# Perceiver layer on one core: the first 512 context rows by seven half-size products instead of eight

## The chip, the cores and the metric

The kernel runs on one core of one Trainium2 chip. Its time is the device time of one execution in microseconds (us), as the median of several runs. The engines are called as the profile calls them: PE (TensorE, matrix products), PEld (its weight loads), DVE (VectorE), ACT (ScalarE), POOL (GpSimd) and SP (SyncE, which issues most DMAs here). All values are 32-bit floats. The profile counts every matrix product of that type as two matmul records; "record" below means one of the two.

## The reference, cut to what matters

One layer is computed on 256 tokens of width 512 (`x`): cross attention with 4096 further context rows, then a state-space block, then a mixture of 32 experts. Only the first part is touched:

```python
xn   = layernorm(x)                                  # 256 x 512
q    = rope(rms_norm(xn @ wq)); k0 = rope(rms_norm(xn @ wk)); v0 = xn @ wv
k_c  = rms_norm(h_ctx_kv @ wk_ctx)                   # 4096 x 512: 4 heads of 128
v_c  = h_ctx_kv @ wv_ctx                             # 4096 x 512
out  = softmax(q [k0; k_c]^T / sqrt(128), causal on the first 256) [v0; v_c] @ wo
```

The context is worked through in eight steps of 512 rows. In each step a 512 x 512 block of context is multiplied by the two 512 x 512 matrices `wk_ctx` and `wv_ctx`, side by side a 512 x 1024 matrix.

## The kernel before

**Two ways to multiply a context step.** Steps 1 to 7 (`fast_steps`, line 398) use Winograd's form of Strassen's method, in two levels: both matrices are cut into halves each way, and seven products of halves take the place of eight, at the price of sums of blocks ahead of them and of results behind them. Step 0 (`context_pieces`, line 310) multiplies plainly: per 128 rows one `key_piece` and one `value_piece`, each four products of 128x128 by 128x512 accumulated in one PSUM bank (`project`, line 222), 32 products in all. A key piece is copied out by ACT, its squares are summed by ACT (`head_squares`) for the norm, and TensorE turns it (`key_transpose`, line 299). The norm factor is not multiplied into the key but used as the scale of the later exponential (this is the `bounded` arm of the program, the one that runs).

**The opening.** SP issues the loads of the first context block `ctx0`, of `wk_ctx` (`wkc`), `x`, the rest of `ctx0` and `wv_ctx` (`wvc`); then, behind a branch, `wk`, `wq`, `wv` and two further context blocks. While they land, PE makes three key pieces, turns the layer-normed `xn` (`turn_xn`, line 213; DVE copies the result to `xT`, line 220), makes a value piece and goes on to the self blocks.

**The self blocks.** `self_block` (line 562) makes 512 columns of k or q for 128 tokens: eight records on PE into one of two `ps_mm` banks; ACT copies them to one of two `raw` buffers (line 536) and sums squares; DVE does the rotary embedding in four instructions (lines 541 to 544); POOL raises the norm factor to the power -1/2 (line 200) and multiplies it in (line 545); DVE transposes 32x32 blocks (line 268) and DMAs put them in place. The two blocks of `wq[3]` are turned by PE instead (line 575). There are ten such blocks. One list after line 607 sets the order in which they, the value pieces and the transposes are written; a planner then gives each engine the earliest-written instruction that it takes to be ready, so the order can shift a little. Each engine works its queue in order.

**Sums of the weights.** The fast steps need T1, T2 and T4, sums of quarters of the weights. POOL makes them in three instructions of 128x1024 (`weight_sums`, lines 338 to 340) once `wvc` is there. The fourth, T3, is formed in place in `wvc` by DVE (`last_sum`, line 389) in the middle of the attention to the layer's own tokens, when the value pieces of step 0 no longer need `wvc`; POOL then makes four further sums of it (`second_sums("wv")`, lines 379 to 382).

**Attention.** `bounded_attention` (line 652) goes through the sources s = 0 (own tokens), 1 (context step 0) to 8. Beside s = 1 run the products of context step 1, and so on, so each step is ready before it is attended to.

Of the kernel before, what the change touches and what calls it, by code (L numbers as in the profile page):

```python
# [11 lines left out]
FP = mybir.dt.float32  # L12
# [7 lines left out]
P = 128  # L20
# [55 lines left out]
def perceiver_layer(ctx: ExitStack, tc: tile.TileContext, a: dict, out: bass.AP):  # L76
# [24 lines left out]
    load_wkc(1, 1)  # L101
    load_wkc(2, 2)
    nc.sync.dma_start(x_sb, a["x"].rearrange("(t p) d -> p t d", p=P))
    load_ctx0(1, 1)
    load_ctx0(2, 2)
    nc.sync.dma_start(wvc, a["wv_ctx"].rearrange("(k p) n -> p k n", p=P))

# [33 lines left out]
    def layer(ctx, bounded):  # L141
# [71 lines left out]
        def turn_xn(t, tp, halves=False):  # L213

            for k in range(KD):
                TE.transpose(tp[:, k * P:(k + 1) * P], xn[:, t, k * P:(k + 1) * P], ident)

            for copy, ks in (((V.tensor_copy, slice(0, KD // 2)), (S.copy, slice(KD // 2, KD))) if halves else
                             ((V.tensor_copy, slice(0, KD)),)):
                copy(xT[:, ks, t * P:(t + 1) * P], tp.rearrange("p (k n) -> p k n", k=KD)[:, ks])  # L220

# [20 lines left out]

        ctx_tiles = {0: ctx0}

        def load_ctx(c):
            ct = ctxp.tile([P, CK // P, KD, P], FP, tag="ctx", name="ctx")
            nc.sync.dma_start(ct, a["ctxT"][c])
            ctx_tiles[c] = ct

        wk = wpiece(a["wk"], "wk")  # L250
        wq = [wpiece(a["wq"][:, 0:512], "wq0")]
        wv = wpiece(a["wv"], "wv")
        wq += [wpiece(a["wq"][:, j * 512:(j + 1) * 512], f"wq{j}") for j in range(1, 4)]
        load_ctx(1)

# [31 lines left out]
        def context_tiles(c):  # L287

            kT = kvp.tile([P, NKV, CK], FP, tag="kT", name="kT")
            v = kvp.tile([P, CK // P, NKV * HD], FP, tag="v", name="v")  # L290
            r = small.tile([P, CK // P, NKV], FP, tag="rk", name="rk", bufs=2)
            kv[c + 1] = (kT, v, r)
            raws = {}

            def key_transpose(i):
                tp = ps_tp.tile([P, NKV, P], FP, tag="tp", name="kTp")
                raw = raws.pop(i)
                for h in range(NKV):
                    TE.transpose(tp[:, h, :], raw[:, h, :], ident)

                if bounded:
                    S.copy(kT[:, :, i * P:(i + 1) * P], tp)
                else:
                    S.activation(kT[:, :, i * P:(i + 1) * P], tp, AF.Copy, scale=kw_col)

            def key_blocks(i):
                turn_heads(kT[:, :, i * P:(i + 1) * P], raws.pop(i), kd[c][i])
            return v, r, raws, key_transpose, key_blocks

        def context_pieces(c):  # L310

            ct = ctx_tiles.pop(c)
            v, r, raws, key_transpose, _ = context_tiles(c)

            def key_piece(i):
                ps = ps_mm.tile([P, 512], FP, tag="mm", name="ps_k")
                project(ps, lambda k: ct[:, i, k, :], lambda k: wkc[:, k, :])
                raws[i] = raw = krp.tile([P, NKV, HD], FP, tag="kraw" if i == 1 else "kn", name="kraw")
                S.copy(raw, ps.rearrange("p (h d) -> p h d", d=HD))
                key_rms(raw, r[:, i, :])  # L320

            def value_piece(i):
                ps = ps_mm.tile([P, 512], FP, tag="mm", name="ps_v")
                project(ps, lambda k: ct[:, i, k, :], lambda k: wvc[:, k, :])
                S.copy(v[:, i, :], ps)

            return [[lambda i=i, f=f: f(i) for i in range(CK // P)] for f in (key_piece, value_piece, key_transpose)]

# [54 lines left out]

        def last_sum():

            V.tensor_tensor(b12, b22, b12, ALU.subtract)
            each(second_sums("wv"))  # L390

        three = ring([(ps_mm, "mm"), (ps_mm, "mm"), (ps_tp, "tp")] if bounded else [(ps_mm, "mm")])

        def fast_steps(c, behind=None):
# [19 lines left out]
            def sums():  # L414
# [3 lines left out]
                G.tensor_tensor(S2, S1, a11, ALU.subtract)  # L418
                left("P6", S2)
                G.tensor_tensor(S3, a11, a21, ALU.subtract)  # L420
                left("P7", S3)
# [108 lines left out]

        heads_done = []

        def norm_rope(ps, t, tb):
# [9 lines left out]
            V.tensor_tensor(u[:, :, HALF:HD], raw[:, :, 0:HALF], sn[:, :, HALF:HD], ALU.mult)  # L543
            V.tensor_tensor(o, o, u, ALU.add)
            heads_done.append(G.tensor_tensor(o, o, r.unsqueeze(2).to_broadcast([P, REP, HD]), ALU.mult).ins)
# [5 lines left out]
        kv[0] = (kT0, v0, None)  # L551
        ctx_k, ctx_v, ctx_t = context_pieces(0)
        for t in range(NT):
            normed = layernorm(t)
        for i in range(3):
            ctx_k[i]()
        for t in range(NT):
            turn_xn(t, ps_sc.tile([P, 512], FP, tag="sc", name="lnT"))
        rope_table(tab_k, kw_bc)
        rope_table(tab_q, qw_bc)  # L560
        with tc.issue_after(normed.ins):
# [25 lines left out]
        q = [[lambda j=j, t=t: q_of(j, t) for t in range(NT)] for j in range(4)]  # L587
        turns = ctx_t[0:3]

        def last_key():  # L590
            ctx_k[3]()
            return ctx_t[3]

# [3 lines left out]
        def behind_head(group, n=1):  # L597
            with tc.issue_after(heads_done[-1]):
                for _ in range(n):
                    next(early[group])  # L600

        weights_of = lambda: next(placed)
        one, two = lambda: behind_head("t"), lambda: behind_head("t4", 2)
        for f in (ctx_v[0], lambda: k_of(0), lambda: k_of(1), last_key, *q[0], ctx_v[1], weights_of, lambda: self_value(0),
                  q[1][0], one, q[1][1], one, lambda: self_value(1), weights_of, q[2][0], one, q[2][1], one, ctx_v[2],
                  q[3][0], two, q[3][1], two, ctx_v[3]):
            turn = f()
            if f not in (weights_of, one, two):
                turns.append(turn)
            while len(turns) > 2:  # L610
                turn = turns.pop(0)
                if turn:
                    turn()
# [19 lines left out]
        pin(nc.sync.dma_start(by_channel, a["by_channel"]))  # L633
        pin(nc.sync.dma_start(by_head, a["by_head"].partition_broadcast(P)))

# [16 lines left out]
        def bounded_attention(beside):  # L652

            pp = pool("pp", 4)
            bq = small.tile([P, 3], FP, tag="bq", name="bq", bufs=1)
            V.tensor_reduce(bq[:, 0:1], qw_bc, AX.X, ALU.max, apply_absolute_value=True)
            V.tensor_reduce(bq[:, 1:2], kw_bc, AX.X, ALU.max, apply_absolute_value=True)
            shift = bq[:, 2:3]
# [49 lines left out]
            for s in range(NC + 1):  # L708
# [12 lines left out]
                for n, st in enumerate(steps):  # L721
                    if s == 0 and n == 3:
                        for turn in turns:
                            turn()
                    if s == 0 and n == 8:
                        with tc.issue_after(masked[-1]):
                            last_sum()
                    pending.append((*st, scores(*st)))
# [19 lines left out]
        def general_attention():  # L748
            with ExitStack() as gctx:
# [12 lines left out]
                for turn in turns:  # L762
                    turn()
                last_sum()

                for s in range(NC + 1):
# [1048 lines left out]
```

## Time and profile before

| what | value |
|---|---|
| runs | 960.70, 960.75, 959.02 us; median 960.7 |
| the profiled execution | 961.0 us, of which the span of the profile is 959.2 |
| busy over the span | PE 98%, DVE 60%, POOL 45%, ACT 40% |
| granted TensorE clock | 0.998 of full |
| first matmul record of PE | at 5.45 us |
| first score of the attention | at 79.34 us |
| first product of context step 1 | at 101.14 us |

Times are counted from the start of the span. In a line of the timeline the first number is the start, the second the duration of a merged group of equal instructions, "x8" their number, and what stands in brackets is the idle time of the engine ahead of it and what ended it. Full-size matmul records overlap in the listing: each is shown with 592 ns, though the next begins 429 ns later.

### The profile page before, as it was taken

To read this page: it belongs to the slowest core of one execution; us is meant where nothing else is said; L and a number is where in the kernel's file an instruction comes from. 1 tells how busy PE (TensorE), PEld (TensorE's weight loads), DVE (VectorE), ACT (ScalarE), POOL (GpSimd) and SP (SyncE) were. 2 spreads that over 40 slices of the span, in tenths; PEclk is the share of its full clock that TensorE was granted. 3 is DMA by queue.
4 is the path that set the end of the run, shared out by engine and by line. 5 is a ranking of instruction groups with operands and counts; after the bars stand their busy time and mean duration, and the time that the engine had idled before them with its cause. 6 is when DMAs were issued, how large, how long until landed. Compare 5 with 4: busy or idle time off the path is not lost.

```text
span 959.2 us, 10117 instructions
## 1 busy us (share of the span) xinstructions
PE 939.9 (98%) x3025; PEld 508.0 (53%) x3025; DVE 571.4 (60%) x1205; ACT 383.0 (40%) x872; POOL 429.3 (45%) x487
## 2 busy tenths in 40 slices
PE   7999999999999999999999999999999999999996
PEld 3444555555555555555555555544465655555442
DVE  4458766566566656665756656658497666632223
ACT  3646444344344444343443444443253742122221
POOL 3559956345444644634724723300013234545542
PEclk9999999999999999999999999999999999999999
DMA  9732053053034015104205203360046453899983
GB/s 328 241 78 47 0 176 87 1 154 89 1 86 141 15 35 174 35 14 152 77 1 153 67 1 88 81 228 0 0 157 209 165 196 122 327 328 366 362 322 109
DMA packets 130803, 124.93 MB, mean 130 GB/s; under 512 B 80017, under 2 KB 99250, under 8 KB 125490
## 3 DMA queue, kind: packets, MB, share of 16 engines
q1 hardware_dynamic: 119216, 77.96, 26.9%
q0 software_dynamic: 7904, 40.90, 11.7%
q10 hardware_dynamic: 3618, 5.33, 1.5%
q8 instruction: 26, 0.43, 0.2%
q14 instruction: 39, 0.32, 0.1%
HBM read 88.76 MB, written 35.41 MB: 129 GB/s over the span
## 4 chain that ended last, share of the span: by engine, by line
PE 95%; issue 1%; POOL 1%; DVE 1%; DMA 1%; ACT 0%; SPq 0%; POOLq 0%; DVEq 0%
PE oT L693 24%; PE scT L668 24%; PE ps_kv L459 15%; PE ps_egu L225 5%; PE ps_self L225 4%; PE ps_v L225 2%; PE ps_o L892 2%; PE ps_xbc L225 2%; PE ps_k L225 2%; PE ps_ye L1616 2%; PE ps_out L1089 1%; PE ps_z L225 1%; PE ps_sgu L225 1%; PE ps_ye L1619 1%; PE xgTp L1495 1%
## 5 line engine op out<-in xcount | busy, mean ns | idle before, releaser
L684 DVE TENSOR_TENSOR lacc<-lacc,prT 128x512 f32<-128x512 f32 x256 | 200.6, 785 | 197.3 <-ACT prT L674 196.2
L674 ACT ACTIVATE prT<-scT,bq,rk 128x512 f32<-128x512 f32 x256 | 198.4, 775 | 280.4 <-PE scT L668 269.5
L668 PE MATMUL scT<-qT,kT 128*128 128x512 f32 x536 | 273.5, 592 | 0.0
L693 PE MATMUL oT<-prT,v 128*128 128x512 f32 x528 | 269.4, 592 | 0.1
L693 PEld LDWEIGHTS oT<-prT,v 128*128 128x128 f32 x528 | 100.1, 190 | 125.8 <-issue 117.9
L668 PEld LDWEIGHTS scT<-qT,kT 128*128 128x128 f32 x536 | 101.2, 190 | 41.0 <-issue 30.6
L459 PE MATMUL ps_kv<-fast,ctx 128*128 128x256 f32 x350 | 99.6, 379 | 0.0
L459 PEld LDWEIGHTS ps_kv<-fast,ctx 128*128 128x128 f32 x350 | 66.4, 190 | 48.3 <-issue 39.9
L410 POOL TENSOR_TENSOR ctx<-ctx 128x128 f32<-128x128 f32 x21 | 11.4, 542 | 98.7 <-PE ps_kv L459 98.7
L200 POOL TENSOR_TENSOR rk<-pv,mhalf 128x4 f32<-128x4 f32 x32 | 37.4, 1180 | 28.0 <-DVE pv L199 28.0
L262 ACT ACTIVATE xn<-kraw 128x128 f32<-128x128 f32 x112 | 33.5, 301 | 39.4 <-POOL kraw L434 22.1
L459 PE MATMUL ps_kv<-wkv,ctx 128*128 128x256 f32 x168 | 48.9, 379 | 0.0
L444 POOL TENSOR_TENSOR v<-fast,v 128x768 f32<-128x768 f32 x21 | 40.9, 1960 | 16.2 <-DVE fast L488 15.6
L459 PEld LDWEIGHTS ps_kv<-wkv,ctx 128*128 128x128 f32 x168 | 31.8, 190 | 28.4 <-issue 25.0
L699 DVE TENSOR_TENSOR oacc<-oT,oacc 128x512 f32<-128x512 f32 x64 | 43.6, 682 | 0.0
L1599 DVE TENSOR_TENSOR hid<-si,ps_egu 128x128 f32<-128x128 f32 x18 | 5.2, 287 | 47.5 <-ACT si L1597 47.5
L459 PE MATMUL ps_kv<-fast,fast 128*128 128x256 f32 x112 | 33.3, 379 | 0.0
L459 PEld LDWEIGHTS ps_kv<-fast,fast 128*128 128x128 f32 x112 | 21.3, 190 | 17.8 <-issue 12.0
L268 DVE STREAM_TRANSPOSE tr<-kraw 128x512 f32<-128x512 f32 x28 | 18.3, 690 | 19.6 <-POOL kraw L433 19.6
L892 PE MATMUL ps_o<-wo,qT 128*128 128x512 f32 x64 | 28.8, 592 | 0.0
L1290 POOL DMA_INDIRECT xg_sb<-xg,place x16 | 15.1, 947 | 29.1 <-PE xgTp L1495 26.7
L225 PE MATMUL ps_self<-wq,xT 128*128 128x512 f32 x64 | 28.1, 592 | 0.0
(439 smaller groups left out, 1412.8 us busy)
## 6 DMA issues: line engine op xcount, KB each, us to landing
xg<-xn SPq DMA_DIRECT2D x6, 2560.0 KB, 9.4
ctx<-in_ctxT_dram SPq DMA_DIRECT2D x7, 1024.0 KB, 5.0
kd<-tr SPq DMA_DIRECT2D x112, 64.0 KB, 2.2
kT<-kd SPq DMA_DIRECT2D x28, 256.0 KB, 3.0
ye<-y_sb ACTq DMA_DIRECT2D x19, 256.0 KB, 8.3
wq<-in_wq_dram SPq DMA_DIRECT2D x4, 1024.0 KB, 14.4
wo<-in_wo_dram SPq DMA_DIRECT2D x4, 1024.0 KB, 7.9
w_in<-in_W_inT_dram SPq DMA_DIRECT2D x4, 1024.0 KB, 8.7
```

The costliest lines, as they stand in the source:

```text
L200: return G.tensor_tensor(dst, v[:, :n], mhalf[:, :n], ALU.pow)
L225: TE.matmul(ps, lhs(k), rhs_of(k), start=(k == 0), stop=(k == KD - 1))
L262: S.activation(sq[:, h, :], raw[:, h, :], AF.Square, accum_out=ss[:, h:h + 1])
L444: G.tensor_tensor(to[:, 1:4], q, base[:, 1:4], ALU.add)
L459: TE.matmul(b[n], sets[name][i], y, start=start, stop=True, skip_group_check=True)
L668: scored.append(TE.matmul(sc, kT[:, g, i * P:(i + 1) * P], qT[:, t, heads4(g), :].rearrange("p h q -> p (h q)"), start=True, stop=True).ins)
L674: S.activation(pr, sc, AF.Exp, bias=shift, scale=SCALE if r is None else r[:, i, g:g + 1])
L684: V.tensor_tensor(la, la, pr, ALU.add)
L693: TE.matmul(outs[g, t], v[:, i, g * HD:(g + 1) * HD], pr, start=(n == 0), stop=last)
L699: V.tensor_tensor(ov, outs.pop((g, t)), ov, ALU.add)
L892: TE.matmul(m["ps_o", t], aT[:, t, h, :], wo[j][:, h % 4, :], start=(h == 0), stop=(h == NH - 1))
L1616: TE.matmul(ps[i], h[:, i, :], wd[i], start=True, stop=False)
```

## The change

Step 0 also uses seven products of halves, but in one level only. With the context block cut into a11, a12 (rows 0 to 255), a21, a22 (rows 256 to 511) and the weights into b11, b21 (`wkc`) and b12, b22 (`wvc`), the new `first_step` forms

- S1 = a21 + a22, S2 = S1 - a11, S3 = a11 - a21, S4 = a12 - S2 on DVE, in a tile `first_sums` that is taken from the two context buffers;
- P1 = a11 b11 and P2 = a12 b21 (their sum is the key of rows 0 to 255, and P1 is also copied out by ACT), P6 = S2 T2, P7 = S3 T3, P4 = a22 T4, P5 = S1 T1, P3 = S4 b22, each as two groups of two products of 128x128 by 128x512.

Ten additions on DVE (one operand in PSUM, one in SBUF) put the results together. P1 and P2 come first, in the opening; the turns of their two keys are written behind the first and the second self block; P6, P7, P4 and the pair P5, P3 are written into the list of self blocks in the places where value pieces stood. T3 is formed behind the rotary embedding of the fourth self block. The turns of keys use the score banks (`ps_sc`, three) in place of the one `ps_tp` bank.

The opening loads become: `ctx0` rows 0 to 127, `wkc` quarters 0 and 1, `ctx0` rows 128 to 255, `x`, `wkc` quarters 2 and 3, and behind the branch the other half of `ctx0`, `wk` in two halves, `wvc`, then as before. Because `first_sums` holds a context buffer, the load of context step 2 moves from the opening to a place behind the load of `by_head`, at the beginning of s = 1. The rotary tables, the sums S1 to S4 and two small reductions are queued behind the copy of `xT`. `second_sums("wv")` is written among the sums of context step 1.

```diff
     load_wkc(1, 1)
-    load_wkc(2, 2)
+    load_ctx0(1, 1)
     nc.sync.dma_start(x_sb, a["x"].rearrange("(t p) d -> p t d", p=P))
-    load_ctx0(1, 1)
-    load_ctx0(2, 2)
-    nc.sync.dma_start(wvc, a["wv_ctx"].rearrange("(k p) n -> p k n", p=P))
+    load_wkc(2, 1)
+    load_wkc(3, 1)
...
+        load_ctx0(2, 2)
+        wk = wpool.tile([P, KD, 512], FP, tag="w", name="wk")
+        for k in (0, 2):
+            nc.sync.dma_start(wk[:, k:k + 2, :], a["wk"][k * P:(k + 2) * P, :].rearrange("(k p) n -> p k n", p=P))
+        nc.sync.dma_start(wvc, a["wv_ctx"].rearrange("(k p) n -> p k n", p=P))
...
+            def product(ps, lhs, rhs, j, start=True):
+                for k in range(2):
+                    TE.matmul(ps, lhs[:, j, k, :], rhs[:, k, :], start=(start and k == 0), stop=(k == 1),
+                              skip_group_check=True)
+                return ps
...
+            def p1(j):
+                x[j] = product(bank(True), a11, b11, j)
+                S.copy(v[:, j, :], x[j])
+
+            def p2(j):
+                product(x[j], a12, b21, j, False)
+                S.copy(flat(key(j)), x.pop(j))
+
+            def p6(j):
+                V.tensor_tensor(v[:, j, :], product(bank(), S2, T2, j), v[:, j, :], ALU.add)
+
+            def p7(j):
+                V.tensor_tensor(v[:, 2 + j, :], product(bank(), S3, b12, j), v[:, j, :], ALU.add)
+
+            def p4(j):
+                V.tensor_tensor(flat(key(2 + j)), product(bank(), a22, T4, j), v[:, 2 + j, :], ALU.add)
+                return key_done(2 + j)
+
+            def p5(j):
+                z[j] = product(bank(True), S1, T1, j)
+                V.tensor_tensor(v[:, 2 + j, :], z[j], v[:, 2 + j, :], ALU.add)
+
+            def p3(j):
+                product(z[j], S4, b22, j, False)
+                V.tensor_tensor(v[:, j, :], z.pop(j), v[:, j, :], ALU.add)
+
+            def sums12():
+                V.tensor_tensor(S1, a21, a22, ALU.add)
+                V.tensor_tensor(S2, S1, a11, ALU.subtract)
+
+            def sums34():
+                V.tensor_tensor(S3, a11, a21, ALU.subtract)
+                V.tensor_tensor(S4, a12, S2, ALU.subtract)
...
-        for i in range(3):
-            ctx_k[i]()
+        for f in (p1, p2) if bounded else ():
+            for j in range(2):
+                f(j)
...
+        with tc.issue_after(turned.ins):
+            key_turns = [key_done(j) for j in range(2)] if bounded else []
+            rope_table(tab_k, kw_bc)
+            rope_table(tab_q, qw_bc)
+            sums12()
+            sums34()
...
-        for f in (ctx_v[0], lambda: k_of(0), lambda: k_of(1), last_key, *q[0], ctx_v[1], weights_of, lambda: self_value(0),
-                  q[1][0], one, q[1][1], one, lambda: self_value(1), weights_of, q[2][0], one, q[2][1], one, ctx_v[2],
-                  q[3][0], two, q[3][1], two, ctx_v[3]):
+        for f in (*of_heads[0:1], *key_turns[0:1], *of_heads[1:2], *key_turns[1:2], *q[0], weights_of,
+                  lambda: self_value(0), last_first, q[1][0], one, *both(p6), q[1][1], one, lambda: self_value(1), weights_of,
+                  *both(p7),
+                  q[2][0], one, q[2][1], one, *both(p4), q[3][0], two, q[3][1], two, *both(p5), *both(p3)):
...
-            while len(turns) > 2:
+            while len(turns) > 3:
...
-                    if s == 0 and n == 8:
-                        with tc.issue_after(masked[-1]):
-                            last_sum()
```

## The prediction, made before the changed kernel had run

> **What bounds the kernel now.** I read the page first: busy tenths in 40 slices, then the chain of work that ended last.
>
> ```profile
> PE   7999999999999999999999999999999999999996
> ...
> PE 95%; issue 1%; POOL 1%; DVE 1%; DMA 1%; ACT 0%; SPq 0%; POOLq 0%; DVEq 0%
> ```
>
> PE is busy in every slice and the chain is PE's own queue. A matmul record that goes away shortens the span by its pitch, unless PE then waits for something. So I looked at the stretches around the change, and at what PE waits for in the first 100 us:
>
> ```profile
> 5.45:17.87 12.42, 12.42 (x26) 5.52 (x27) 5.93 (x21) 5.56 (x19) 2.15 (x3) 1.00 1.02 367
> 17.87:79.34 61.47, 61.47 (x164) 28.26 (x163) 34.79 (x62) 34.15 (x121) 36.42 (x32) 1.00 0.58 167
> 79.34:101.14 21.80, 21.69 (x55) 9.12 (x54) 19.04 (x23) 14.94 (x24) 21.54 (x21) 1.00 0.18 40
> ```
>
> ```profile
> PE ps_k L225 <- DMA wkv<-in_wk_ctx_dram: 5.4, 1, 5.4
> ```
>
> Columns of the first: stretch, its length, then busy time and count of PE, PEld, DVE, ACT, POOL, the granted clock, the DMA share, GB/s. From 5.45 us on PE has no idle time until the attention; its one wait is the first load. DVE and POOL have 35 and 36 us of work in the 61 us of the self blocks, so there is room, but they take turns in one chain per block. The timeline shows the pitch and the ends that matter:
>
> ```profile
> 5.45 12.42 PE L225 MATMUL ps_k<-wkv,ctx 128*128 128x512 f32 x24 [5.45 <-DMA wkv<-in_wk_ctx_dram]
> ...
> 65.17 3.60 PE L225 MATMUL ps_v<-wkv,ctx 128*128 128x512 f32 x8
> 68.61 7.03 PE L225 MATMUL ps_self<-wq,xT 128*128 128x512 f32 x16
> 75.47 3.60 PE L225 MATMUL ps_v<-wkv,ctx 128*128 128x512 f32 x8
> ...
> 79.34 2.74 PE L668 MATMUL scT<-qT,kT 128*128 128x512 f32 x6
> ...
> 82.89 0.60 PE L575 MATMUL selfT<-ident,lacc 128*128 128x128 f32 x4
> ```
>
> From 65.17 to 68.61 eight records take 3.44 us, 0.43 each. In the opening 24 records take 12.42 us, 2.1 more than 24 x 0.43: the first five come at about 0.86. The changed kernel starts with the same first loads, so it pays that too.
>
> **The change, part by part.**
>
> *Products.* Removed: 32 products, 64 records. Added: 7 x 2 x 2 = 28 products, 56 records of the same shape. Net 8 records, -3.44 us of PE, all in the stretch where PE never waits. This is the whole gain there is.
>
> *Opening, PE.* Before: 24 key records, then the turn of xn. After: 16 records (P1, P2), which at the same pitches end at 17.87 - 8 x 0.43 = 14.4. P2 accumulates on a bank that ACT must first have copied out, and ACT's first copy is late:
>
> ```profile
> 11.09 1.28 ACT L319 ACT_TABLE_LOAD   x1 [11.09 <-DMA tables<-in_tables_dram]
> ```
>
> (The load named there is put down by time; PE's first group ended just before.) P1's first half ends near 9.2; 1.28 for the table and 0.59 for the copy (the row behind it, at 12.38) later is 11.1, and P2 would start at 10.8: +0.3. Bounds 0 (the table comes earlier) and +2.1 (it does wait for that load, copy done at 12.97).
>
> *Turn of xn.* Before, a value piece covered DVE's copy to `xT`. After, the next block in the list needs it: four turns, then a copy of 0.68, about 0.5 idle. The turn of key 0 (0.44 on PE, ready after its copy near 13.8) can slip into that gap, as the planner let such a turn slip behind the first records of a self block before. I take +0.1; bounds 0 and +0.5.
>
> *Opening loads.* Same bytes up to `wvc`, other order.
>
> ```profile
> wk<-in_wk_dram SPq DMA_DIRECT2D x1, 1024.0 KB, 13.8
> ```
>
> The last number is the time from issue to landing. `wk` was issued at 5.72 and landed 13.8 later, at 19.5; `wvc`, in the place ahead, landed just before POOL's first weight sum at 16.92. They change places: `wk`'s second half by 16.9, and it is needed by the fifth record of the first self block, near 16.0 + 1.7 = 17.7: cost 0, hidden by 0.8 us; without that cover up to +1.9 (if it came at 19.6). `x` moves ahead of 256 KB and stays early; `wkc`'s last quarters take the places near 9 to 10 us, before 10.8. SP issues two DMAs more and one less (0.4 each), ahead of what waits for buffers anyway: 0. The load of context step 2 leaves the opening for about 88 us, behind `by_head` on SP, which nothing follows until 122; DMA share is 0.18 there, and step 2 is used after 150: 0, the cover being some 60 us.
>
> *Sums on DVE and POOL.* `weight_sums` waits for `wvc`: 19.5 to 26.7 in place of 16.9 to 24.3. T2 is first used by P6 near 38, T1 and T2 copies behind the k blocks: 0 on PE. But DVE now has S1 to S4 (four of 128x512; 0.69 each by the rotary row of that size) and the first rotary block in that stretch, and DVE and POOL hold each other up:
>
> ```profile
> 17.10 2.30 DVE L199 TENSOR_SCALAR pv<-ss 128x4 f32<-128x4 f32 x2
> ...
> 52.26 0.69 DVE L541 TENSOR_TENSOR lacc<-raw,oacc 128x512 f32<-128x512 f32 x1 [4.11 <-ACT raw L536]
> ...
> 55.69 1.49 DVE L541 TENSOR_TENSOR lacc<-raw,oacc 128x512 f32<-128x512 f32 x1 [1.27 <-ACT raw L536]
> ...
> 105.27 0.41 DVE L468 TENSOR_TENSOR fast<-ps_kv,fast 128x256 f32<-128x256 f32 x1
> ```
>
> Two small DVE instructions (0.13 to 0.16 each elsewhere) lasted until POOL's first weight sum, 16.92 to 19.31, had ended. The rotary instruction took 1.49 beside POOL's multiply and 0.69 alone. An addition from PSUM takes 0.41 even where POOL works 18.9 of 20 us, and is not held. So I let three DVE instructions (S3, S4, the first rotary one) each wait for one weight sum, S1 and S2 being done by 19.6: block k0's rotary part then ends at 28 + 0.7 + 0.35 + 0.35 + 0.6 = 30 instead of 22.5. Its `raw` buffer is free at 29.3, the third block's copy ends at 29.9, and PE needs that bank for the first self value at 30.8. Cost 0 with 0.9 us to spare; bounds 0 and +3.2 (the slower rival).
>
> [...]
>
> *Ten additions on DVE* (0.68, a copy from PSUM of that size, line 697, to 2 x 0.41): 6.8 to 8.2 us, and T3's 1.48 moved forward. DVE goes from 35 to about 47 of some 60 us; four ACT copies of 0.59 fewer. P6, P7 and P4 use the three score banks, idle here: 0. P5 and P3 share `ps_mm`: P3 waits until DVE has added P5. At the end of the list P4 also gives ACT eight squares (2 x 1.9 us) ahead of the copies of the last two q blocks, and DVE's additions queue behind their rotary parts, which took up to 3.3 us beside POOL (76.3 to 79.6). The last q block ended on PE at 75.47, POOL's multiply for it at 82.77, 7.3 us later, and its turn ran at 82.89. After: two key turns, P5, the other turn and the first half of P3 follow that block, 3 x 0.43 + 3 x 1.72 + 0.2 = 6.6. So the turn stalls 0.7 to 1, if it keeps its place ahead of the last half of P3; before, three scores covered it. I take +0.8; bounds 0 and +2.3.
>
> *Attention.* T3 leaves DVE there (1.48) and `second_sums("wv")` was worked by POOL at 103 to 111 already: 0. POOL's sums for context step 1 finished for its first product at 94.4, used at 101.14; 2 us less still leaves 4.
>
> Sum: -3.44 + 0.3 + 0.1 + 0 + 0.8 = -2.2. The profiled execution took 961.0 (959.2 span and 1.8 around it), 0.3 above the median of the runs, 960.7. 960.7 - 2.2 = 958.5. Later stretches move along: PE's waits after 100 us are ten of at most 0.7 us, none for a load.
>
> **The rivals.** A change of 0.2% is 1.9 us, about what a measurement of this kernel can tell from none: 958.8 to 962.6 counts as no change.
>
> *Full gain*: the last stalls vanish (the planner puts the last turn behind P3) and only the 0.3 stays: 960.7 - 3.1 to 3.4, 957.3 to 957.6. For it: PE had no stall at all in this stretch; against: the 7.3 us lag.
>
> *Gain eaten*: the end of the list costs its bound 2.3, the gap at `xT` 0.5, the first copy 0.3 and the bank near 31 us 0.5: -3.44 + 3.6 = +0.2, 960.9. For it: each is one engine's lag already seen; against: they overlap in part, a PE that was late finds the next one ready.
>
> *Slower, one mechanism*: DVE's queue falls behind POOL's weight sums. If more of DVE's instructions are caught (the norm factors of the two keys, 0.13 alone and 2.2 caught, besides S3 and S4), k0's rotary part ends near 34, its bank is free at 34, and PE waits 30.8 to 34; the next bank is late by another 2 for k1, and the lag reaches the end of the list with its 2.3 and 0.3 from the opening. 3.2 + 2 + 2.3 + 0.3 = 7.8, less 3.4, is +4.4: 965. It decides once k0's rotary part ends after 30.2; from about 32.5 on (2.3 there, 2 at the next bank, 0.8 and 0.3 as in the sum, less 3.4: +2.0) it is a loss that counts. For it: POOL starts 2.6 us later than before, right where DVE's new work is; against: only three weight sums exist to be caught by.
>
> **How the numbers follow.** Forecast (stalls of 0.6 to 2.1, 957.9 to 959.4): 0.44. Full gain: 0.16. Gain eaten: 0.19. Slower: 0.21. The predicted time is the forecast's, 958.5. Some two thirds of the forecast (0.30) lies below 958.8, so faster 0.30 + 0.16 = 0.46, same 0.14 + 0.19 = 0.33, slower 0.21. The range goes from 956.9 (the full gain less 0.4 of spread; 0.04 outside) to 964.0 (most of the way to the slower case; 0.14 outside).
>
> **What would show it.** Right: the first score near 77.5 in place of 79.3, 56 records of that shape for step 0, a PE gap of 0.3 ahead of P2 and one under 1 ahead of the last `selfT`. The DVE steps are wrong if PE waits between 30 and 40 us for a copy of ACT; the loads if the first self block waits for `wk`; the end if P3 waits for DVE by over 1 us. The prediction falls if PE gains on the stretch up to 101 us and loses it later, which nothing in this profile shows.

## The result, and the profile after

The changed kernel takes 975.4 us (median of four runs, 974.4 to 975.9) where the kernel before took 960.7 in the same series (959.0 to 960.8): 1.0156 times as long, 95% interval 1.0139 to 1.0174. That is 14.7 us slower. The forecast was 958.5, with a range up to 964.0: it was wrong, and so was the range. The profiled execution took 975.9, of which the span is 974.2; these are 961.0 and 959.2 before. In the experiments further down one execution of e1 (988.1 us) and one of e4 (980.9) fell into a slower state of the chip, and both are left out.

On the page of the changed kernel, the busy tenths and the chain of work that ended last:

```profile
PE   7799799999999999999999999999999999999996
...
PE 87%; DVE 4%; DMA 3%; POOL 3%; ACT 1%; issue 1%; SPq 0%; POOLq 0%; DVEq 0%
```

Two slices (of 24 us each) have fallen from 9 to 7, the second and the fifth, and the chain is no longer 95% PE. The table by stretches has the same columns as in the prediction; its ends are the same events (first record, the same 17.87, first score, first product of step 1):

```profile
5.59:17.87 12.28, 12.27 (x31) 6.04 (x32) 4.63 (x14) 6.23 (x20) 1.19 (x2) 1.00 1.03 376
17.87:87.07 69.20, 62.55 (x156) 27.90 (x155) 48.31 (x84) 32.15 (x119) 44.98 (x37) 0.95 0.47 132
87.07:115.90 28.83, 23.18 (x49) 9.43 (x48) 18.67 (x21) 13.50 (x21) 23.75 (x28) 0.94 0.23 66
```

The first score comes at 87.07 instead of 79.34, the first product of step 1 at 115.90 instead of 101.14. So all the loss, 14.76 us, lies ahead of that product; behind it the two kernels take equally long (the difference of the medians is 14.7). PE is idle for 6.65 us of the second stretch and 5.65 of the third, and the granted clock is down to 0.95 and 0.94 there. What PE waits for in the first 130 us (waited in total, times, longest):

```profile
PE ps_first L385 <- DMA wkv<-in_wk_ctx_dram: 5.6, 1, 5.6
PE scT L730 <- DMA qT<-qd: 5.0, 1, 5.0
PE ps_first L385 <- DVE v L408: 4.6, 1, 4.6
PE ps_first L385 <- DVE pv L198: 1.4, 1, 1.4
PE selfT L633 <- POOL lacc L594: 0.7, 1, 0.7
PE oT L755 <- DVE lacc L739: 0.7, 1, 0.7
```

The first is the opening load, as before. The other five are new, 12.3 us together. Their places on PE's timeline:

```profile
39.43 1.96 PE L385 MATMUL ps_first<-oacc,first_sums 128*128 128x512 f32 x4 [1.36 <-DVE pv L198]
41.22 1.88 PE L225 MATMUL ps_self<-wq,xT 128*128 128x512 f32 x4
47.71 3.78 PE L385 MATMUL ps_first<-oacc,first_sums 128*128 128x512 f32 x4 [4.61 <-DVE v L408]
51.28 2.38 PE L225 MATMUL ps_self<-wq,xT 128*128 128x512 f32 x4
...
84.86 0.65 PE L633 MATMUL selfT<-ident,lacc 128*128 128x128 f32 x4 [0.69 <-POOL lacc L594]
...
103.45 2.07 PE L730 MATMUL scT<-qT,kT 128*128 128x512 f32 x2 [4.97 <-DMA qT<-qd]
```

The two halves of P6 are torn apart: the first (39.43) waits 1.36, four records of a q block slip in, and the second (47.71) waits 4.61. Its four records then take 3.78 where the first half's took 1.96: behind the long gap they come 0.85 apart instead of 0.43. The score at 103.45 waits 4.97, and its two records take 2.07 instead of 1.02.

The sum of the loss: the five waits, 12.3; slow records behind the gap at 47.71 (the eight up to 53.50 took 5.79 instead of 3.43), 2.4; behind the gap at 103.45 (four in 3.52 instead of 1.72), 1.8; the opening, in which the first seven records instead of the first four or five come at 0.85, 1.0 in this execution, and a start 0.15 later. That is 17.7, and the eight records saved take 3.4 off: 14.3 of the 14.8.

Who is late? The same execution on the other engines:

```profile
37.39 0.69 DVE L426 TENSOR_TENSOR first_sums<-ctx 128x512 f32<-128x512 f32 x1
...
42.00 1.05 ACT L308 COPY kT<-kTp 128x512 f32<-128x512 f32 x2
...
46.98 0.68 DVE L408 TENSOR_TENSOR v<-ps_first,v 128x512 f32<-128x512 f32 x1
...
94.16 0.70 DVE L274 STREAM_TRANSPOSE tr<-lacc 128x512 f32<-128x512 f32 x1
...
100.66 0.38 SPq L279 DMA_DIRECT2D qT<-qd  x1
```

- *Stall of 1.4, P6's first half.* S1 (line 426) starts at 37.39, though its rows of context had landed at 12.34. S1 to S4 stand in DVE's queue inside the rotary part of the third self block; P6 needs S2, done at 39.3. The name in the list of waits, `pv` L198, is the small instruction that follows S2.
- *Stall of 4.6, P6's second half.* In the program its only wait is for DVE: it was given the bank of the first half, and has to wait until DVE has added that one up. PE had finished it at 41.4; DVE adds it at 46.98, behind the rest of one rotary part, T3 and most of the next. The other two score banks were taken by the turned keys 0 and 1, which PE had made at 16.26 and 23.74 and ACT copied out only at 42.00.
- *Stall of 5.0, a score.* The second block of `q[2]` was ready on POOL at 74.5. DVE turned it (line 274) at 94.16, after three masks of the attention; the load into `qT` was issued at 100.66, landed at 103.41, and PE had wanted it at 98.5. Before, the same turn ran at 81.80 and the load landed at 89.15, about 1 us ahead of the score that uses it.

That turn and that score in the kernel before:

```profile
81.80 0.70 DVE L268 STREAM_TRANSPOSE tr<-lacc 128x512 f32<-128x512 f32 x1
...
90.20 1.02 PE L668 MATMUL scT<-qT,kT 128*128 128x512 f32 x2
```

All three are instructions that stand late in an engine's queue; none of them takes long itself.

### The profile page after: what moved, and what is told of

Same layout as the page of the kernel before. It is cut to its first block, busy times and chain, and to the rows that moved or that the text cites. A ratio compares the mean times of both kernels' runs of the same rounds, so it can differ in the third digit from the quotient of the medians.

```text
span 974.2 us, 10117 instructions
## 1 busy us (share of the span) xinstructions
PE 942.3 (97%) x3017; PEld 508.7 (52%) x3017; DVE 579.5 (59%) x1219; ACT 380.3 (39%) x868; POOL 425.3 (44%) x487
## 4 chain that ended last, share of the span: by engine, by line
PE 87%; DVE 4%; DMA 3%; POOL 3%; ACT 1%; issue 1%; SPq 0%; POOLq 0%; DVEq 0%
PE oT L755 23%; PE scT L730 23%; PE ps_kv L508 15%; PE ps_egu L225 5%; PE ps_o L949 2%; PE ps_xbc L225 2%; PE ps_ye L1673 2%; PE ps_first L385 2%; PE ps_out L1146 1%; PE ps_z L225 1%; PE ps_sgu L225 1%; PE ps_ye L1676 1%; DMA yk<-ye,row_y 1%; PE ps_self L225 1%; PE xgTp L1552 1%
## 5 line engine op out<-in xcount | busy, mean ns | idle before, releaser
L746 DVE TENSOR_TENSOR lacc<-lacc,prT 128x512 f32<-128x512 f32 x256 | 197.9, 774 | 200.2 <-ACT prT L736 198.9
L455 POOL TENSOR_TENSOR ctx<-fast 128x128 f32<-128x128 f32 x28 | 19.9, 711 | 19.7 <-PE ps_kv L508 19.3
```

Source lines behind the costliest of these rows:

```text
L455: G.tensor_tensor(s1, x[:, 1, 0], x[:, 1, 1], ALU.add)
L746: V.tensor_tensor(la, la, pr, ALU.add)
```

## The experiments

The first theory, called ORDER in the expectations: the loss is these three places in the queues, and putting them right takes it away. Its rivals: LOCK, that DVE is held by POOL's weight sums and everything else follows; and LOADS, that the new order of the opening loads costs the time itself. Ratios are to the kernel before on the same chip; before had 960.0, 960.4 and 964.8 us on the three chips of e1 to e12 and 960.6 with e13 to e15, so times are compared by these ratios.

### Each stall by itself

**e1.** S1 to S4 are kept in free places (`qT`, `xn`) instead of a context buffer, and are then made early.

```diff
-        first_sums = ctxp.tile([P, CK // P, KD, P], FP, tag="ctx", name="first_sums")
...
-            S1, S2, S3, S4 = carve(first_sums, *[OP] * 4)
+            S1, S2, S3, S4 = (s.rearrange("p (a b) n -> p a b n", a=2) for s in (
+                qT[:, 1, 12:16], qT[:, 1, 4:8], qT[:, 0, 12:16], xn[:, 1].rearrange("p (h n) -> p h n", n=P)))
```

> The changed kernel with S1 to S4 kept in memory that is idle then (three places of the query buffer, one of the normalised rows) and not in the ring of context buffers; the planner then puts the four VectorE sums ahead of the first self key's rotary part, 18 instructions earlier. ORDER theory (three stalls of TensorE, each made by the place that an instruction got in its engine's order: the sums, 1.36 us; the copies of the turned keys, which hold two of three banks, 4.61 us and about 2.4 of slow clock behind it; the turn of the sixth query block, 4.97 us and about 1.7 of slow clock): the wait for the sums goes, but the second P6 still waits for the bank that the add of the first one frees, and this add stands behind the same rotary parts as before, so the 1.36 us are only moved into the second wait: 975.4 +- 1.5. LOCK theory (VectorE is held by the weight sums on GpSimd, 7.3 us in three instructions, and everything behind it is late): four more sums ahead of the first rotary part let it end at 31 instead of 28.5, so 976 to 979.

Measured: 973.8, ratio 1.0131 (1.0111 to 1.0152), at the lower edge of what ORDER gave and below LOCK's. The stall of 1.4 is gone, that of P6's second half is 3.6 instead of 4.6, that of the score stays. One line of its timeline is used further down:

```profile
45.53 3.78 PE L385 MATMUL ps_first<-oacc,qT 128*128 128x512 f32 x4 [3.61 <-DVE v L408]
```

**e5.** The turned keys go back to their own bank.

```diff
-                tp = (ps_sc if bounded else ps_tp).tile([P, NKV, P], FP, tag="sc" if bounded else "tp", name="kTp")
+                tp = ps_tp.tile([P, NKV, P], FP, tag="tp", name="kTp")
```

> The changed kernel with the context keys turned in the bank of the kernel before, and the sums left in the ring of context buffers. The plan then puts the first P6 ahead of the fifth query product and the four sums between the rotary parts of the first query block, four places earlier than in the changed kernel. ORDER theory: the wait for the bank (4.61 and about 2.4 of slow clock) goes; P6 now waits 1 to 3 us for the sums where it waited 1.36; the wait for the sixth query block stays: 968 to 971. LOCK theory: 973 to 976, with the wait moved to P6's sums.

Measured: 971.7, ratio 1.0117 (1.0102 to 1.0133), 0.7 above what ORDER gave and below LOCK's. The wait for P6's first addition is gone, as the account by the bank has it; the wait for S1 to S4 (1.9, named L427, which is S2) stands in its place. Behind that wait PE's records come slowly too, which is used at the end:

```profile
35.58 1.52 PE L385 MATMUL ps_first<-oacc,first_sums 128*128 128x512 f32 x2 [1.90 <-DVE first_sums L427]
36.90 4.91 PE L225 MATMUL ps_self<-wq,xT 128*128 128x512 f32 x8
```

**e2.** Both edits together.

> As e1, and the context keys are turned in the bank that the kernel before used for it (shared with the squares) and not in one of the three score banks, so that both P6 products find a bank. ORDER theory: both waits at P6 (1.36 and 4.61) go, and the slow clock behind the second (about 2.4); the wait for the sixth query block stays: 975.4 - 8.4 = 967.0, 965 to 968.5. LOCK theory: a bank more helps nothing while VectorE is late; the wait moves to the next product that needs VectorE: 973 to 976.

Measured: 968.9, ratio 1.0096 (1.0079 to 1.0113): a little over. Both waits at P6 are gone and the one for `qT` stays (5.2); 1.5 ahead of the last turned block and some of 0.3 to 0.7 are new.

**e3.** The first masks of the attention are queued behind the last `turn_heads` on DVE; nothing else is touched.

```diff
+        turned_heads = []
...
-            V.transpose(tr, src.rearrange("p h d -> p (h d)"))
+            turned_heads.append(V.transpose(tr, src.rearrange("p h d -> p (h d)")).ins)
...
-                    masked.append(V.tensor_tensor(p3, p3, upper.unsqueeze(1).to_broadcast([P, REP, P]), ALU.mult).ins)
+                    with tc.issue_after(turned_heads[-1]):
+                        masked.append(V.tensor_tensor(p3, p3, upper.unsqueeze(1).to_broadcast([P, REP, P]), ALU.mult).ins)
```

> The changed kernel with one edge of order: the masks of the first attention step are issued behind VectorE's turn of the sixth query block, so that this turn comes at about 84 us and not at 94. ORDER theory: the wait of 4.97 us for that block and the slow clock behind it (about 1.7) go and nothing else: 975.4 - 6.7 = 968.7, 967.5 to 970. LOCK theory: the turn is late because VectorE is, so the masks wait in its place and TensorE for the masks: 973 to 977.

Measured: 968.7, ratio 1.0094 (1.0073 to 1.0116). The wait for `qT` is gone and the two at P6 are as in the changed kernel.

**e4.** All three edits.

> e2 and e3 together. ORDER theory: the gains add: 975.4 - 8.4 - 6.7 = 960.3, 958.5 to 962, which is the kernel before within the measurement's bound, since about 2.4 us are left that the change also cost (the opening about 1, the last turns 0.7, the first mask 0.7) against the 3.44 it saves. LOCK theory: 971 or more.

Measured: 962.4, ratio 1.0024 (1.0014 to 1.0034), just over ORDER's 962. The three stalls are gone, and by the ratios 12.7 us with them; smaller waits (1.5 ahead of the last `selfT`, 1.3 ahead of an `oT`, 0.6, 0.6, 0.4) keep it from the time before.

**e8.** e4's edits, and the turn of the very last block written behind P3, so that it stands behind the first scores as it did before the change; P5 in a score bank.

```diff
-                z[j] = product(bank(True), S1, T1, j)
+                z[j] = product(bank(), S1, T1, j)
...
+        last_p3 = both(p3)
...
-                  q[2][0], one, q[2][1], one, *both(p4), q[3][0], two, q[3][1], two, *both(p5), *both(p3)):
+                  q[2][0], one, q[2][1], one, *both(p4), q[3][0], two, q[3][1], two, *both(p5), *last_p3):
             turn = f()
-            if f not in (weights_of, one, two, last_first):
+            if f not in (weights_of, one, two, last_first, *last_p3):
```

> e4 with two more edits of order and bank: TensorE's turn of the eighth query block goes behind the first three score products, as in the kernel before, and P5 takes score banks, so that it does not wait for ScalarE's copies of the last query blocks. ORDER theory: in e4 TensorE still waited 1.5 us for GpSimd at that turn and 0.6 for the two copies; both go: 962.5 - 2.1 = 960.4, 959 to 961.5; at best the kernel before's time, as 1.3 us at a mask and 1.0 at two squares remain. If these small waits are covered elsewhere, it stays at 962.5.

Measured: 960.7, ratio 1.0004 (0.9995 to 1.0013): the time before, as expected. So the three places explain most of the loss (12.7 of the 14.7 us); with the last turn and P5's bank changed too, the rest of it goes. They do not explain why the instructions stand there.

### The lock

**e6.** POOL's three weight sums are made over 64 of their 512 columns and the rest is zero, so T1, T2 and T4, and the products made of them, are left out for the most part; DVE can hardly be held by them.

```diff
-            G.tensor_tensor(t1, b12, b11, ALU.subtract)
-            G.tensor_tensor(t2, b22, t1, ALU.subtract)
-            G.tensor_tensor(t4, b21, t2, ALU.subtract)
+            few = slice(0, 64)
+            G.tensor_tensor(t1[:, :, few], b12[:, :, few], b11[:, :, few], ALU.subtract)
+            G.tensor_tensor(t2[:, :, few], b22[:, :, few], t1[:, :, few], ALU.subtract)
+            G.tensor_tensor(t4[:, :, few], b21[:, :, few], t2[:, :, few], ALU.subtract)
...
+        for rest in sums:
+            G.memset(rest, 0.0)
```

> The changed kernel with GpSimd's three weight sums made over 64 of 512 columns, the rest set to zero early (so the values of P6, P4 and P5 are not those of the reference): VectorE is then not held by them, and the first key's rotary part ends at about 25 us and not at 28.5. LOCK theory (this hold is the cause): the three stalls go with it, 961 to 964. ORDER theory: the whole chain of rotary parts moves some 3 us forward, so the wait for the sums goes (1.36) and the wait for the bank shrinks by 2 to 3, while the sixth query block's turn still stands behind the masks: 968 to 972.

Measured: 967.9, ratio 1.0076 (1.0061 to 1.0092): ORDER's 968 to 972 is met at its lower edge, LOCK's 961 to 964 is missed. PE still waits 1.6 at P6's second half and 5.3 for `qT`. In the changed kernel three DVE instructions lasted 2.65, 2.50 and 2.63 us beside these sums (0.16, 0.28 and 0.42 elsewhere), so the lock makes the queue later by some 7 us (in e6 the rotary part of the first self block ends at 22.07 instead of 28.54), and it takes part in most of what is lost at P6. But with the lock gone half of the whole loss stays, and e4 and e8 come near or back to the time before with the lock in place. LOCK is a part, not the cause.

### Why the instructions stand there: the loads

**e7.** The kernel before with nothing but the new opening loads.

```diff
-    load_wkc(2, 2)
-    nc.sync.dma_start(x_sb, a["x"].rearrange("(t p) d -> p t d", p=P))
     load_ctx0(1, 1)
-    load_ctx0(2, 2)
-    nc.sync.dma_start(wvc, a["wv_ctx"].rearrange("(k p) n -> p k n", p=P))
+    nc.sync.dma_start(x_sb, a["x"].rearrange("(t p) d -> p t d", p=P))
+    load_wkc(2, 1)
+    load_wkc(3, 1)
...
-        wk = wpiece(a["wk"], "wk")
+        load_ctx0(2, 2)
+        wk = wpool.tile([P, KD, 512], FP, tag="w", name="wk")
+        for k in (0, 2):
+            nc.sync.dma_start(wk[:, k:k + 2, :], a["wk"][k * P:(k + 2) * P, :].rearrange("(k p) n -> p k n", p=P))
+        nc.sync.dma_start(wvc, a["wv_ctx"].rearrange("(k p) n -> p k n", p=P))
```

> The kernel before with only the opening loads in the new order (context tile 1 ahead of x, the key weights' last quarters behind it, wk in two halves ahead of wv_ctx). LOADS theory (the new order is what costs): 965 or more. ORDER theory: nothing waits for these loads (wv_ctx lands at 17.9 in the changed kernel and its first product was at 18.6): 959 to 961.5.

Measured: 966.5, ratio 1.0057 (1.0039 to 1.0076). ORDER's number for it was missed: the loads alone cost 5.5 us (the profiled execution, 964.2, shows 3.8 of it). But apart from 0.3 in the opening, what PE newly waits for is no load of the opening:

```profile
PE ps_k L224 <- DMA wkv<-in_wk_ctx_dram: 5.3, 2, 5.0
PE scT L671 <- DMA qT<-qd: 2.6, 1, 2.6
```

The turn of the second `q[2]` block has moved on DVE from 81.80 to 84.66, and the load behind it landed at 93.07 instead of 89.15; 2.5 of these 3.9 us are its later issue, and 1.4 the load itself, which took 4.1 instead of 2.7. The loads of the opening have moved an instruction that runs 70 us later.

**e9.** e7 with e3's edit on top.

> e7 (the kernel before with the new load order) and e3's edit: the masks of the first attention step behind VectorE's turn of the sixth query block. In e7 TensorE waited 2.6 us for that block, whose turn had come at 84.7 instead of 81.8 us, two places later in VectorE's order. ORDER theory: the new loads cost e7 its 5.5 us only by moving that turn in the plan, so they all come back: 959.5 to 961.5. LOADS theory (the transfers themselves are in the way): 964 to 967.

Measured: ratio 1.0016 (1.0000 to 1.0033). The wait for `qT` is gone, and most of the 5.5 us with it. The loads cost mainly by way of the queue on DVE.

**e10.** The changed kernel with the loads of the kernel before (the reverse of e7's diff).

> The changed kernel with the opening loads in the order of the kernel before. In its plan the sixth query block's turn stands behind the first mask, as in the kernel before, and no longer behind the third, and the four sums stand in the second key's rotary part. ORDER theory: the wait for that block goes with its slow clock (6.7) and the wait for the sums (1.36), the wait for the bank stays or grows, and the opening loses 1 to 3 us since context tile 1 lands at 9.9 and the second product of four wants it at 7.3: 967 to 972. LOADS theory (the new order is the cause of the whole loss): 962 or less.

Measured: ratio 1.0007 (0.9992 to 1.0022), that is within the measurement of before, and far below what ORDER gave. (The profiled execution was the longest of eleven, 972.6 where the median is 965.9, with waits of 1.4 to 2.0 us behind 830 us; only its beginning is read here.) PE waits 3.2 in all for loads of the opening, as expected. All three stalls are gone, the one at P6's second half too, which I had put down to the banks: here ACT copies the turned keys at 39.19, and the two halves of P6 run back to back at 41.94, although DVE adds the first one up only at 45.28: they have a bank each.

So the switch is in the loads, and two things are in that edit: the order of the transfers, and that two loads (the second half of `ctx0`, and `wv_ctx`) moved from ahead of the program's branch to behind it. The last three runs take these apart. PLACE is the theory that the branch is the cause, TRANSFERS that the order is.

**e14.** e10, with these two loads written behind the branch. SP issues the same transfers in the same order.

```diff
-    load_ctx0(2, 2)
-    nc.sync.dma_start(wvc, a["wv_ctx"].rearrange("(k p) n -> p k n", p=P))
...
+        load_ctx0(2, 2)
+        nc.sync.dma_start(wvc, a["wv_ctx"].rearrange("(k p) n -> p k n", p=P))
         wk = wpiece(a["wk"], "wk")
```

> The changed kernel with before's order of all opening loads, as in e10, but with the second half of ctx0 and wv_ctx written behind the branch: SP issues the same transfers in the same order as in e10, only the branch stands ahead of two of them. PLACE theory: the three stalls are back (a wait of 4 to 5 us for the query qT, one of 3 to 5 us at P6 or P6 and a q block interleaved, first product of step 1 at 112 to 116), ratio to before 1.010 to 1.017. TRANSFERS theory: as e10, ratio 0.999 to 1.003, no wait for qT.

Measured: 973.7, ratio 1.0131 (1.0115 to 1.0146). Two of the three stalls are back, where PLACE gave all three. The two longest waits of PE behind the opening load, and P6's second half and the score on the timeline:

```profile
PE scT L727 <- DMA qT<-qd: 4.7, 1, 4.7
PE ps_first L382 <- DVE v L405: 3.2, 1, 3.2
```

```profile
46.86 1.99 PE L382 MATMUL ps_first<-oacc,first_sums 128*128 128x512 f32 x4 [3.23 <-DVE v L405]
...
100.02 2.08 PE L727 MATMUL scT<-qT,kT 128*128 128x512 f32 x2 [4.67 <-DMA qT<-qd]
```

S1 starts at 36.53 here (37.39 in the changed kernel) and the turn of the `q[2]` block at 91.06. In e10 S1 stands one self block earlier in DVE's queue, in the rotary part of the second block and not of the third:

```profile
31.13 0.68 DVE L423 TENSOR_TENSOR first_sums<-ctx 128x512 f32<-128x512 f32 x1
```

POOL's first weight sum starts at 16.12, earlier than e10's 16.36, so neither the transfers nor the lock is later than in e10.

**e13.** The changed kernel with only these two loads written ahead of the branch; `wkc` in quarters, `x` and `wk` in halves stay as the change has them.

```diff
     load_wkc(3, 1)
+    load_ctx0(2, 2)
+    nc.sync.dma_start(wvc, a["wv_ctx"].rearrange("(k p) n -> p k n", p=P))
...
-        load_ctx0(2, 2)
...
-        nc.sync.dma_start(wvc, a["wv_ctx"].rearrange("(k p) n -> p k n", p=P))
```

> The changed kernel, with two of its opening loads (the second half of ctx0, and wv_ctx) written ahead of the branch again; wkc's quarters, x and wk in halves stay as in the change. PLACE theory (the loss comes from these two loads standing behind the branch, which moves S1 to S4, the addition of P6 and the last turn of q2 late on VectorE): all three stalls of 1.4, 4.6 and 5.0 us go, first product of step 1 near 102.5, ratio to before 0.998 to 1.001 (958.5 to 961.4 on a before of 960.4). TRANSFERS theory (the new order of the quarters, of x and of wk costs the time): stalls stay, ratio 1.010 to 1.017.

Measured: 960.3, ratio 0.9994 (0.9985 to 1.0003). No stall of the three is left, and the first product of step 1 comes at 100.76. P6's two halves in one row:

```profile
38.27 3.60 PE L385 MATMUL ps_first<-oacc,first_sums 128*128 128x512 f32 x8
```

DVE's timeline, S1 and the turn of the `q[2]` block, and all that PE waits for up to 130 us but the opening load:

```profile
30.65 0.68 DVE L426 TENSOR_TENSOR first_sums<-ctx 128x512 f32<-128x512 f32 x1
...
81.80 0.70 DVE L274 STREAM_TRANSPOSE tr<-lacc 128x512 f32<-128x512 f32 x1
```

```profile
PE oT L755 <- DVE lacc L739: 1.0, 2, 0.5
PE ps_self L227 <- DMA wk<-in_wk_dram: 0.7, 1, 0.7
PE ps_first L385 <- DVE v L419: 0.6, 1, 0.6
PE lnT L217 <- DVE xn L211: 0.3, 1, 0.3
```

S1 is 6.7 us earlier than in the changed kernel, and the turn is at 81.80, the very time that it had before. The lock is still there: two DVE instructions last 2.50 and 2.48 us beside the weight sums, and the rotary part of the first self block ends at 27.12, without a stall. PLACE holds in both directions: 15 us disappear with two lines moved ahead of the branch (where `wv_ctx` also comes ahead of `wk`), and 12 appear with the same two lines moved behind it and all transfers in the same order. What is shown is that the place of these two loads, with the transfers the same, changes the order of the engines' queues, and with it the time. No run puts the two loads later in the program but still ahead of the branch, so whether the branch itself or only the later place does it is not shown. How the planner comes to it was not measured; that it takes what was loaded ahead of the branch as already there, and has its own guess of the arrival of what is loaded behind it, is an inference.

### Is the forecast's gain there once the stalls are gone?

**e15.** e13 with the last turn behind P3, by the last two hunks of e8's diff.

> e13 with P3's second half ahead of the turn of the last q block, which then stands behind the first three scores, where it was before the change. If e13 has lost its stalls and what is left of the forecast's 3.4 us is eaten at the end of the list, the last turn no longer waits, first product of step 1 near 101.5, ratio 0.996 to 1.000. If the turn comes too late for the scores there, a wait of 1 to 3 us stands at a score or at oT instead, ratio 1.000 to 1.003.

Measured: 959.7, ratio 0.9991 (0.9982 to 1.0000). The wait at P3 is unchanged at 0.6, that at `oT` 1.0 in one piece. In this execution the turn of `xn` waited 2.4 for the layer norm, and the first product of step 1 came at 101.60. It cannot be told from e13.

**e11 and e12.** e1's edit; the second `q[2]` block is turned by TensorE instead of DVE and DMAs, which needs no `qT` load at all; the last turn behind P3. The two runs differ in the banks: in e11 the turned keys 2 and 3 use `ps_mm` and P5 a score bank, in e12 these keys use a score bank.

```diff
-            if bounded and w is not wq[3]:
+            if bounded and w is not wq[3] and not (w is wq[2] and t == 1):
                 return turn_heads(dst, o, qd.pop())
...
+                early = bounded and w is wq[2]
+                tp = (ps_sc if early else ps_tp).tile([P, REP, P], FP, tag="sc" if early else "tp", name="selfT")
```

> e8 with the sixth query block turned by TensorE as the last two are (a score bank, 0.43 us of TensorE more) and the late context keys turned in product banks. In e8 TensorE waited 1.8 us for that block's way through memory and 1.75 for the squares that share the keys' bank. ORDER theory: both go and 0.4 comes: 960.7 - 3.5 + 0.4 = 957.6, and up to 1 us of new wait for the product bank of the last query block: 957 to 959, faster than the kernel before by 0.2%. If other small waits take their place: 960 to 961.

> As e11, but the late context keys are turned in score banks and P5 keeps the product banks, where e4 showed two waits of 0.36 and 0.23 us for ScalarE's copies: 957 to 959 by ORDER theory, 960 to 961 if other waits take the place of those removed.

Measured: ratios 1.0018 (1.0006 to 1.0030) and 1.0030 (1.0011 to 1.0049), both missed. The wait for `qT` is gone, but PE now waits 2.9 ahead of the new turn, for POOL's multiply. In e11 the turn runs at 68.75 and the next eight records of a q block, which stand behind it, start at 69.49: on PE the turn waits for the same chain that the DMAs had covered.

No kernel beat the one before by more than it can be measured; e13 and e15 equal it.

## Why the prediction was wrong, point by point

- **"S1 and S2 being done by 19.6": failed.** It was taken from when data and engine would be free. S1 ran at 37.39. The prediction had put a cost on how long DVE's new instructions would be held, and none on where in the queue they would be put. This is 1.4 at P6's first half.
- **"P6, P7 and P4 use the three score banks, idle here: 0": failed**, by 4.6 and 2.4 of slow records. The same diff had put the turned keys into these banks, and two of the three stayed taken until ACT's copy at 42.00. The description of the change names the move; the prediction did not count the banks. That it could have been 0 is shown by e13: the copies run at 36.66, and the halves of P6 follow each other at 38.27 although DVE adds the first up only at 44.79.
- **"Attention: 0", "later stretches move along": failed**, by 5.0 and 1.8. The load behind the turn of the second `q[2]` block had about 1 us to spare before the change. The prediction looked at the last block, which PE turns, and not at the one that goes through DVE, SP and two DMA hops.
- **Opening loads, 0: failed in its reasoning.** As transfers they cost nothing: `wk`'s halves landed at 13.85 and 15.19 (by 16.9 was forecast) and PE waits for none of them. But the edit moved two loads across the branch, and that is what moved the places above: 1.0131 against 1.0007 in e14 and e10. For the moved loads the prediction counted the DMAs and their place on SP, and not that all other queues are planned anew around them.
- **The rival "slower, one mechanism" had the sign and not the mechanism.** Its condition was the end of k0's rotary part after 30.2; it ended at 28.54, and PE had no wait for an ACT copy. The lock that it is built on is there and adds to the queue (e6): three DVE instructions were held, as counted, but not the ones counted. S1 to S4 met no weight sum, since they ran from 37.39 on and the sums had ended at 27.2.
- **Products, -3.44: right.** P7's eight records take 3.43, and in the sum of the loss these eight must be taken off.
- **ACT's first copy, +0.3, and the gap at `xT`, +0.1: right within their bounds.** The 16 records run without a gap, in 9.95 us from 5.60 on; the table load (1.28 at 9.44) lay under them. The opening lost 1.0 by slower first records instead, which no step had.
- **POOL's sums from 19.5 to 26.7:** 18.06 to 27.2. Right at the end, 1.4 early at the start.
- **The last `selfT`, +0.8:** 0.69. Right. P3 does not wait for DVE by more than 1.
- **A wait's second cost was left out altogether:** behind the two long gaps 4.2 us went into slow records, on top of 9.6 of waiting. No rival had it.

With the queues in good order, what was left of the forecast's -2.2? e13 has -0.6 (interval -1.4 to +0.3). Its small waits are 2.6 instead of the 1.2 of the sum: 0.7 for `wk`, which the prediction had covered by 0.8 with the transfers in the other order, 0.6 at P3, 1.0 at two `oT` of the attention and 0.3 at the layer norm. So even without the stalls the gain is eaten, as in the rival of that name, but mostly by other waits than the ones that it listed.

## What to carry to other kernels

Where a planner sets the order of the queues, an edit to one load is an edit to every queue: a place such as "S1 is done by 19.6" has to be read from the order that the program was given, not from when the data is there. Before a forecast, list the chains that have some 1 us or less to spare at their end (here one turn on DVE, a DMA out, a DMA in), and ask of each whether anything may be put ahead of it. And count banks by how long each is held, from PE's write to the copy that frees it, not by whether they look idle.

## What the runs showed of the hardware

The price of a gap on PE is not its length alone. Behind gaps of 3.61 us (e1), 4.61 and 4.97 (the changed kernel) and 4.67 (e14) the records come 0.85 apart instead of 0.43 from the first one on, for some 3 to 6 us. In the changed kernel the granted clock was 0.50 from 47.71 to 51.10 and 1.00 from 52.50 to 55.00; it was 0.51 from 103.45 to 106.90 and 1.00 from 106.97 to 108.50. Shorter gaps can do it too: in e5 a gap of 1.90 is followed, from the second record on, by records 0.81 to 0.85 apart, and the granted clock is 0.50 from 36.1 to 39.5; slow records also followed gaps of 2.22 (e10, 16 in 8.80 instead of 7.03), 2.62 (e7, two in 1.36 and the next two in 1.91 instead of 1.02 each) and 2.93 (e11 and e12, eight in 5.04 and 5.29 instead of 3.60). But behind 3.23 (e14) four records took 1.99, the usual 1.88 and a tenth, and the clock stayed at 1.00; so it did behind 1.78 (e8, two records in 1.13 instead of 1.02) and 1.56 (e6, four in 1.98). So the length of a single gap does not decide it in these runs.

A load of 256 KB into `qT` took 2.6 to 2.9 us from issue to landing in the changed kernel, and 4.21 in e8, where PE waited 1.8 for it. The 1 MB load of context step 2, issued 1.4 us behind it in e8, does not explain it by itself: e7's load took 4.12 without such a load behind it, and the changed kernel's and e13's took 2.75 and 2.79 with one 1.5 us behind. What made it slow stays open.
